# Deformable layer of a four-layer kernel: the first sampling weights are made before the branch, and the first window load is issued from two queues

## The chip, the core and the metric

The kernel runs on one core of a Trainium2 chip as one launch. The metric is the device time of that launch in microseconds (us): 5652.51 us before the change, the median of three runs (5646.67, 5652.51 and 5653.47). A difference of about 0.2% is the smallest that a measurement of this kernel can tell from none.

## What is computed

The reference takes an image batch `x` of shape (2, 128, 128, 128) and adds four layers to it in turn, each behind a normalisation: an axial attention, a scan of nine-tap convolutions in four directions, a deformable 3x3 convolution, and a convolution in a Hadamard-transformed form. Only the third is touched. Cut to what matters:

```
offset, mask = split(conv2d(x, w_off, b_off))      # 27 maps: 9 taps x (dy, dx), and 9 masks
py = off_y + ky + hh ;  px = off_x + kx + ww       # where each tap of each pixel reads
sampled = bilinear(x, py, px) * sigmoid(mask)      # (B, Cin, 9, H, W)
out = einsum('bckhw,ock->bohw', sampled, w) + b    # 3x3 weights, summed over channels and taps
```

## The kernel before, in words

The four layers run one after the other. An image stays in SBUF as `res[n]`, channels on the partitions. The deformable layer (`layer2`, L1166) has two stages and a branch between them.

**Offsets** (`layer2_offsets`, L1180). It first loads the small weights `woff` and `boff` and writes zeros around the padded image `px_d` in HBM with eight transfers, all of them issued by ScalarE's queue (ACT, L1191 to L1205); then it computes the group normalisation, whose square root is on ScalarE too (L45), behind these issues. Then 16 blocks of 16 rows follow: ScalarE normalises the rows into `gx` (L1224), TensorE makes the 27 offset maps (`ps_off`, 36 matmuls, L1236), the maps are transposed (`pt`, `ot`) and written to `off_d` in HBM by SyncE's queue (SP, L1260), the normalised rows are transposed too and written to `px_d`, channels last (L1270). VectorE (DVE) keeps the largest and smallest offset. At the end `far` (L1285) tells whether any offset is beyond 2.

**Branch** (L1173). All five engines read `far` and compare. With far offsets `layer2_gather` would run; with the inputs of this kernel the other side, `layer2_windows`, does.

**Windows** (`layer2_windows`, L1288). The work is 128 halves: 2 images x 32 groups of 4 rows x 2 half-rows of 64 pixels. For a half, ten transfers of 80 KB on SP's queue load `xw`, 16 windows of 10x10 pixels with all channels (L1320), and an eleventh loads the offsets `o` (L1322). From `o` and the constant `base` VectorE and ScalarE make the hats: `hats` (DVE), `hatted` (ACT: Abs, then Relu), `masked` (DVE). Each half is then done in two parts `b`. For a part, `outer` (DVE) multiplies the hats of y and x into `w`, `turn` (PE, nine transposes) and `turned` (DVE copy) bring it to `s`, `sample` (PE, eight matmuls) applies `s` to the windows, `sampled` (ACT copies) brings the samples to `sm`, and `convolve` (PE) multiplies them by `wdef`; `finish` (DVE) adds the result to `res`.

The order within an engine is written by hand: every operation of this stage is recorded through `InOrder` (L73), whose line L81 therefore stands for all of them, and tile names tell them apart. In part `b` the code asks first for `turn` and `turned` of part `b+1` and `outer` of part `b+2`, then, in even parts, for `hats` of the half after the next, and only then for `sample` of part `b`. Each engine takes its instructions strictly in that order: a VectorE instruction that waits for a transfer holds all VectorE instructions behind it.

A transfer is issued under one of eight semaphores, used in turn; an issue waits until the last transfer under the same semaphore has landed, so at most eight transfers of this kind are in flight.

Ahead of the loop come the loads of halves 0 to 2, the hats of halves 0 and 1, and the first `outer`, `turn` and `turned`, in this order:

```
loads = {at: load(at) for at in range(3)}
for at in range(2):
    ds[at] = hats(loads[at][1]); hatted(ds[at]); masked(ds[at], loads[at][1])
w = outer(ds[0], 0); ps_w = turn(w); s = turned(ps_w); w = outer(ds[0], 1)
```

Of the kernel before, what the change touches and what calls it, by code (L numbers as in the profile page):

```python
# [7 lines left out]
F32 = mybir.dt.float32  # L8
I32 = mybir.dt.int32
AF = mybir.ActivationFunctionType  # L10
ALU = mybir.AluOpType
# [1154 lines left out]
def layer2(env, prm, res, mem, tables, st_gn, st_next):  # L1166


    nc, tc = env.nc, env.tc
    with tc.tile_pool(name="l2f", bufs=1) as fp:  # L1170
        far = fp.tile([1, 1], I32, name="far", tag="far")
        layer2_offsets(env, prm, res, mem, st_gn, far)
        is_far = nc.values_load(far[0:1, 0:1])  # L1173
        with tc.If(is_far > 0) as branch:
            layer2_gather(env, prm, res, tables, st_gn, st_next)
        with branch.Else():
            layer2_windows(env, prm, res, mem, st_next)


def layer2_offsets(env, prm, res, mem, st_gn, far):  # L1180
# [5 lines left out]
    with ExitStack() as ctx:  # L1186
# [29 lines left out]
        for n in range(N):  # L1216
            for h in range(0, S, NR):
# [56 lines left out]
                at += 1  # L1274

# [12 lines left out]
def layer2_windows(env, prm, res, mem, st_next):  # L1288

    nc, tc = env.nc, env.tc
    ident = env.ident
    with ExitStack() as ctx:
        cp = ctx.enter_context(tc.tile_pool(name="l2d", bufs=1))
        sp = ctx.enter_context(tc.tile_pool(name="l2s", bufs=2))
        pp = ctx.enter_context(tc.tile_pool(name="l2qs", bufs=1, space=PSUM))
        pe, dve, act = (InOrder(tc, e) for e in (nc.tensor, nc.vector, nc.scalar))
        wdef = cp.tile([P, 9, P], F32, name="wdef", tag="wdef")  # L1300
        nc.scalar.dma_start(out=wdef, in_=prm["wdef"])
        bdef = cp.tile([P, 1], F32, name="bdef", tag="bdef")
        nc.scalar.dma_start(out=bdef, in_=prm["bdef"])
        base = cp.tile([P, 18, 10], F32, name="base", tag="base")
        nc.scalar.dma_start(out=base, in_=prm["base2"])

        px = mem["px"]
        halves = [(n, g, hf) for n in range(N) for g in range(NT) for hf in range(2)]

        def load(at):  # L1310
            n, g, hf = halves[at]
            xw = sp.tile([100, 16, P], F32, name="xw", tag="xw", bufs=4)
            for y in range(10):
                here = px[n, g * RT + y, hf * 64 : hf * 64 + 10, :]
                src = bass.AP(
                    tensor=here.tensor,
                    offset=here.offset,
                    ap=[[P, 10], [4 * P, 16], [1, P]],
                )
                nc.sync.dma_start(out=xw[10 * y : 10 * y + 10], in_=src)  # L1320
            o = sp.tile([P, 2, 27], F32, name="o", tag="o", bufs=4)
            nc.sync.dma_start(out=o, in_=mem["off"][n, g, :, 2 * hf : 2 * hf + 2, :])  # L1322
            return xw, o

        def hats(o):
            d = sp.tile([P, 2, 18, 10], F32, name="d", tag="d")
            dve.tensor_tensor(
                d,
                o[:, :, 0:18].unsqueeze(3).to_broadcast([P, 2, 18, 10]),
                base.unsqueeze(1).to_broadcast([P, 2, 18, 10]),  # L1330
                ALU.add,
            )
            return d

        def hatted(d):
            act.activation(d, d, AF.Abs)
            act.activation(d, d, AF.Relu, bias=1.0, scale=-1.0)

        def masked(d, o):
            rows = d.rearrange("p b (k a) s -> p b k a s", a=2)[:, :, :, 0, :]  # L1340
            dve.tensor_tensor(
                rows, rows, o[:, :, 18:27].unsqueeze(3).to_broadcast([P, 2, 9, 10]), ALU.mult
            )

        def outer(d, b):
            w = sp.tile([P, 9, 10, 10], F32, name="w", tag="w")
            v = d[:, b].rearrange("p (k a) s -> p k a s", a=2)
            dve.tensor_tensor(
                w,
                v[:, :, 0, :].unsqueeze(3).to_broadcast([P, 9, 10, 10]),  # L1350
                v[:, :, 1, :].unsqueeze(2).to_broadcast([P, 9, 10, 10]),
                ALU.mult,
            )
            return w

        def turn(w):
            ps = pp.tile([100, 9, P], F32, name="ps_w", tag="ps_w")
            for k in range(9):
                pe.transpose(ps[:, k, :], w[:, k].rearrange("p y x -> p (y x)"), ident)
            return ps  # L1360

        def turned(ps):

            s = sp.tile([100, 8, 36, 4], F32, name="s", tag="s")
            dve.tensor_copy(
                s.rearrange("p t k c -> p k t c"),
                ps.rearrange("p k (r t c) -> p (k r) t c", r=4, t=8),
            )
            return s

        def sample(xw, s, b):
            ps = pp.tile([P, 3, 512], F32, name="ps_s", tag="ps_s")
            for t in range(8):
                pe.matmul(
                    ps[:, t // 3, (t % 3) * 144 : (t % 3) * 144 + 144],
                    lhsT=xw[:, 8 * b + t, :],
                    rhs=s[:, t].rearrange("p k c -> p (k c)"),
                    start=True,
                    stop=True,
                )  # L1380
            return ps

        def sampled(ps, sm, b):
            for j in range(3):
                nt = (3, 3, 2)[j]
                lo = 8 * b + 3 * j
                act.copy(
                    sm.rearrange("p k (t c) -> p k t c", c=4)[:, :, lo : lo + nt, :],
                    ps[:, j, 0 : nt * 144].rearrange("p (t k c) -> p k t c", t=nt, c=4),
                )  # L1390

        def convolve(sm, po, taps):
            for k in taps:
                pe.matmul(
                    po,
                    lhsT=wdef[:, k, :],
                    rhs=sm[:, 4 * k : 4 * k + 4, :],
                    start=(k == 0),
                    stop=(k == 8),
                )  # L1400

        def finish(at, po):
            n, g, hf = halves[at]
            here = res[n][:, g * RT : g * RT + RT, hf * 64 : hf * 64 + 64]
            dve.scalar_tensor_tensor(here, po, bdef[:, 0:1], here, ALU.add, ALU.add)
            if hf == 1:
                dve.bn_stats(
                    st_next[:, n, g, :],
                    res[n][:, g * RT : g * RT + RT, :].rearrange("p h w -> p (h w)"),
                )  # L1410

        count = len(halves)
        loads = {at: load(at) for at in range(3)}
        ds = {}
        for at in range(2):
            ds[at] = hats(loads[at][1])
            hatted(ds[at])
            masked(ds[at], loads[at][1])  # L1420
        w = outer(ds[0], 0)
        ps_w = turn(w)
        s = turned(ps_w)
        w = outer(ds[0], 1)
        sms, pos = {}, {}
        for b in range(2 * count + 2):
            at, part = b // 2, b % 2
            if part == 0 and at + 3 < count:
                loads[at + 3] = load(at + 3)
            if part == 0 and at < count:  # L1430
                sms[at] = sp.tile([P, 36, 64], F32, name="sm", tag="sm")


            s_now = s
            if b + 1 < 2 * count:
                ps_w = turn(w)
                s = turned(ps_w)
                if b + 2 < 2 * count:
                    w = outer(ds[(b + 2) // 2], b % 2)
            if at + 2 < count:  # L1440
                if part == 0:
                    ds[at + 2] = hats(loads[at + 2][1])
                else:
                    masked(ds[at + 2], loads[at + 2][1])
            if b < 2 * count:
                ps_s = sample(loads[at][0], s_now, part)
                sampled(ps_s, sms[at], part)
                if part == 0 and at + 2 < count:
                    hatted(ds[at + 2])
            if at >= 1:  # L1450
                if part == 0:
                    pos[at - 1] = pp.tile([P, RT, 64], F32, name="po", tag="po_w", bufs=2)
                convolve(sms[at - 1], pos[at - 1], range(0, 5) if part == 0 else range(5, 9))
                if part == 1:
                    finish(at - 1, pos.pop(at - 1))
                    sms.pop(at - 1), loads.pop(at - 1), ds.pop(at - 1)
# [621 lines left out]
```

## Time and profile before

| | us |
|---|---|
| median of three runs | 5652.51 |
| lowest and highest | 5646.67, 5653.47 |
| the profiled execution's own time | 5645.21 |
| its span, first to last instruction | 5643.4 |
| TensorE (PE) busy in the span | 5270.7 |
| offsets stage: first `woff` issue to `far` | 3819.86 to 3999.98 |
| windows stage: first transfer to the last `hats` | 4006.53 to 5260.8 |

How to read the views. A row of the timeline gives the start, the duration, the engine (PE for matmuls, PEld for weight loads, DVE, ACT, POOL; a `q` behind the name is the queue that issues a transfer), the line, the operation, the tiles as out<-in, the shape, how many such instructions follow each other, and in brackets how long the engine had been idle and what ended that. An f32 matmul leaves two records, a transpose one. A row of the stretches gives a window, then each engine's busy time with its instruction count, the TensorE clock that was granted (1.00 is full speed), the busy share of the DMA engines and GB/s.

### The profile page before, as it was taken

Reading aid. Unit: us, or ns where it says so; the run is one execution under the profiler, and the core shown is the slowest. Engines: PE = TensorE matmul, PEld = TensorE weight load, DVE = VectorE, ACT = ScalarE, POOL = GpSimd, SP = SyncE. Lnnn points to the kernel's source line nnn. Section 1 sums busy time; section 2 is a strip of 40 time slices with the busy share of each in tenths; the row PEclk is TensorE's granted clock in tenths of the full one; section 3 lists DMA queues with packets and bytes.
Section 4 is the critical chain, followed back from the end, with each engine's and each line's share of the span. In section 5 each row is a group of like instructions: output and inputs, shape, how many; then the busy total and the mean of one; then the engine's idle time right before and its main releaser. Section 6 shows DMA issues by size and latency. Waiting matters only on the chain. (4 is left out here: it accounts for less than half of the span.)

```text
span 5643.4 us, 164496 instructions
## 1 busy us (share of the span) xinstructions
PE 5270.7 (93%) x68347; PEld 4712.5 (84%) x68347; DVE 3697.0 (66%) x7127; ACT 2648.5 (47%) x7896; POOL 1549.2 (27%) x1169
## 2 busy tenths in 40 slices
PE   8997999999999904999999999999799999999999
PEld 8866888888888704999999999994599999999877
DVE  3645888888888854555555556663466666666698
ACT  1046988898888865443223331003233333333322
POOL 2113666666666622000000002330000000000376
PEclk9998999999999957999999999999899999999999
DMA  3243333333333393000000000103577767777211
GB/s 147 97 186 115 60 59 60 61 62 62 60 60 60 72 377 137 1 1 1 2 1 1 1 1 31 46 24 111 107 88 87 86 90 86 88 89 86 49 50 57
DMA packets 413963, 403.75 MB, mean 72 GB/s; under 512 B 63520, under 2 KB 368544, under 8 KB 402336
## 3 DMA queue, kind: packets, MB, share of 16 engines
q1 hardware_dynamic: 404000, 365.18, 32.0%
q10 hardware_dynamic: 9216, 27.95, 1.3%
q8 instruction: 548, 8.98, 0.7%
q14 instruction: 199, 1.63, 0.1%
HBM read 252.31 MB, written 140.68 MB: 70 GB/s over the span
## 5 line engine op out<-in xcount | busy, mean ns | idle before, releaser
L81 PE MATMUL pl<-ln,wl 128*128 128x128 f32 (+1 forms) x10160 | 1240.6, 276 | 30.5 <-DVE ln L81 30.4
L81 PEld LDWEIGHTS pl<-ln,wl 128*128 128x128 f32 x10160 | 1176.2, 190 | 41.4 <-issue 27.0
L81 ACT ACTIVATE e<-e,mx 128x128 f32<-128x128 f32 x2048 | 793.4, 395 | 0.8 <-DVE mx L81 0.8
L81 ACT COPY sm<-ps_s 128x432 f32<-128x432 f32 (+1 forms) x768 | 318.4, 487 | 801.5 <-PE ps_s L81 801.5
L81 POOL TENSOR_TENSOR e<-e,total 128x1024 f32<-128x1024 f32 x256 | 485.9, 1898 | 476.0 <-DVE total L81 465.5
L81 ACT COPY res<-ln 128x128 f32<-128x128 f32 x762 | 262.3, 344 | 719.2 <-DVE ln L81 719.2
L81 PE MATMUL ps_s<-s,xw 100*128 100x144 f32 x4096 | 546.4, 287 | 0.6 <-ACT sm L81 0.6
L81 POOL TENSOR_TENSOR res<-ln,x1t 128x128 f32<-128x128 f32 x256 | 134.4, 525 | 1494.1 <-DVE ln L81 1494.1
L81 DVE COPY s<-ps_w 100x1152 f32<-100x1152 f32 x256 | 346.4, 1353 | 301.7 <-PE ps_w L81 301.7
L81 PE MATMUL po<-sm,wdef 128*128 128x256 f32 x2304 | 539.1, 379 | 0.0
L81 PE MATMUL pl<-ln,ws 128*128 128x128 f32 x4064 | 536.8, 273 | 0.0
L81 POOL COPY et<-et 128x1024 f32<-128x1024 f32 x256 | 516.9, 2019 | 35.3 <-DVE et L81 27.1
L81 PEld LDWEIGHTS ps_s<-s,xw 100*128 100x128 f32 x4096 | 518.2, 191 | 1.1 <-ACT sm L81 1.1
L81 DVE TENSOR_TENSOR v<-pl,c 128x128 f32<-128x128 f32 x508 | 148.1, 291 | 538.4 <-PE pl L81 538.4
L81 PEld LDWEIGHTS pl<-ln,ws 128*128 128x128 f32 x4064 | 494.5, 190 | 0.0
L81 ACT ACTIVATE r<-gen,alphas 128x1536 f32<-128x1536 f32 x256 | 395.0, 1543 | 171.5 <-PE gen L81 142.7
L81 PEld LDWEIGHTS po<-sm,wdef 128*128 128x128 f32 x2304 | 419.8, 190 | 47.6
L81 POOL MEMSET col<- 128x10 f32 (+1 forms) x72 | 5.9, 122 | 1477.4 <-DVE res L81 1469.9
L81 ACT ACTIVATION_READ_ACCUMULATOR e<-e,mx 128x1 f32 x2048 | 396.1, 193 | 0.0
L81 DVE SCALAR_TENSOR_TENSOR ln<-v,res 128x128 f32<-128x128 f32 x1016 | 343.5, 338 | 49.2 <-DVE v L81 1.2
L81 PE MATMUL te<-cst_main,e 128*128 128x128 f32 x2048 | 338.5, 288 | 24.5 <-POOL e L81 17.3
L81 DVE COPY et<-te 128x512 f32<-128x512 f32 x512 | 348.1, 680 | 11.5 <-PE te L81 10.9
(241 smaller groups left out, 9351.8 us busy)
## 6 DMA issues: line engine op xcount, KB each, us to landing
xw<-px_d SPq DMA_DIRECT2D x1280, 80.0 KB
xa<-in_x SPq DMA_DIRECT2D x16, 1024.0 KB
v_d<-vs SPq DMA_DIRECT2D x16, 1024.0 KB
qb_d<-sb SPq DMA_DIRECT2D x16, 1024.0 KB
qa_d<-sa SPq DMA_DIRECT2D x8, 2048.0 KB
zz<-qb_d SPq DMA_DIRECT2D x1024, 16.0 KB
vt<-v_d SPq DMA_DIRECT2D x64, 256.0 KB
qk<-qa_d SPq DMA_DIRECT2D x256, 64.0 KB
```

Source lines behind the costliest of these rows:

```text
L81: return lambda *a, **k: self.tc.keep_in_program_order(issue(*a, **k))
```

## The change

`layer2_windows` becomes a class `Windows` with three steps. Its constructor runs at the head of `layer2` and holds the tiles that live on both sides of the branch. `begin` is called in the offsets stage, behind the code of its fourth block. `turn_first` stands between the offsets and the read of `far`. `run` is the old stage without what was moved.

```diff
-        layer2_offsets(env, prm, res, mem, st_gn, far)
+        windows = Windows(env, prm, fp)
+        layer2_offsets(env, prm, res, mem, st_gn, far, lambda: windows.begin(mem))
+        windows.turn_first()
         is_far = nc.values_load(far[0:1, 0:1])
...
+                if at == 4:
+                    then()
...
+    def __init__(self, env, prm, fp):
+        self.o = [fp.tile([P, 2, 27], F32, name=f"o{k}", tag=f"o{k}") for k in range(2)]
+        nc.scalar.dma_start(out=self.base, in_=prm["base2"])
+        nc.scalar.dma_start(out=self.wdef, in_=prm["wdef"])
+        nc.scalar.dma_start(out=self.bdef, in_=prm["bdef"])
...
+    def begin(self, mem):
+        for at in range(2):
+            self.env.nc.sync.dma_start(
+                out=self.o[at], in_=mem["off"][0, 0, :, 2 * at : 2 * at + 2, :]
             )
         for at in range(2):
+            self.hatted(self.hats(at, self.o[at]))
+            self.masked(self.d[at], self.o[at])
+        for b in range(2):
+            self.outer(self.d[0], b)
+
+    def turn_first(self):
+        with self.env.tc.tile_pool(name="l2q0", bufs=1, space=PSUM) as pp:
+            self.turned(self.turn(pp, self.w[0]), 0)
...
-                nc.sync.dma_start(out=xw[10 * y : 10 * y + 10], in_=src)
+                    queue = nc.scalar if at == 0 and y % 2 else nc.sync
+                    queue.dma_start(out=xw[10 * y : 10 * y + 10], in_=src)
+                if at < 2:
+                    return xw, self.o[at]
```

The loop over the parts is the same; it starts with `s` and the second `w` at hand. The tiles `d`, `w` and `s` were taken from pools of two buffers and are now two named buffers each. `layer2_gather` takes `wdef` and `bdef` from the class and has fewer buffers; it does not run here.

In the built program the two `o` loads stand on SP's queue behind the `px_d` write of the first block; the six VectorE and four ScalarE instructions of `begin` stand behind the fourth block's copies on VectorE and behind the sixth block's `gx` on ScalarE; the nine transposes of `turn_first` are TensorE's last work ahead of the branch, and its copy is VectorE's last, behind `far`. The loads of `base`, `wdef` and `bdef` stand ahead of `woff`, `boff` and the eight zero writes on ScalarE's queue, under the same eight semaphores: the fourth to eighth zero write then wait for `base`, `wdef`, `bdef`, `woff` and `boff` to land. Behind the branch VectorE has, in order: the copy to `s` of part 1, `outer` of part 2, `hats` of half 2 (which waits for half 2's `o`, the 31st transfer of the stage), the copy to `s` of part 2, `outer` of part 3.

## The prediction on record

> **What bounds the kernel now.** The page says first that TensorE (PE) is busy 93% of the span, so what counts is where it isn't. The line of slices has one such place past the middle, near 4000 us, the seam between offsets and windows. Two stretches, asked for by time, show it:
>
> ```profile
> PE 5270.7 (93%) x68347; PEld 4712.5 (84%) x68347; DVE 3697.0 (66%) x7127; ACT 2648.5 (47%) x7896; POOL 1549.2 (27%) x1169
> ...
> 3999.00:4035.50 36.50, 4.31 (x19) 3.59 (x20) 5.68 (x10) 2.01 (x4) 0.00 (x0) 0.50 0.67 143
> 4035.50:4060.00 24.50, 23.95 (x160) 22.34 (x159) 14.55 (x17) 9.04 (x21) 0.00 (x0) 0.92 0.53 52
> ```
>
> In the first PE works 4.31 of 36.5 us, at half clock (0.50); from the second on it is full, and the stretches from 4060 to 5260 us give 1199.57 of 1200 us. So the windows are PE-bound, at 9.8 us a half, and what starts them earlier ends the kernel earlier. The timeline of the seam, DVE, SP and PE rows taken out:
>
> ```profile
> 3999.84 0.14 DVE L1285 CAST far<-m 1x1 int32<-1x1 f32 x1
> 4006.53 0.34 ACTq L1301 DMA_DIRECT2D wdef<-in_wdef  x1
> 4006.56 9.40 SPq L1320 DMA_DIRECT2D xw<-px_d  x10
> 4016.00 0.35 SPq L1322 DMA_DIRECT2D o<-off_d  x1
> 4016.40 4.55 SPq L1320 DMA_DIRECT2D xw<-px_d  x10
> 4019.72 0.53 DVE L81 TENSOR_TENSOR d<-o,base 128x360 f32<-128x360 f32 x1 [19.74 <-DMA xw<-px_d]
> 4025.83 0.53 DVE L81 TENSOR_TENSOR d<-o,base 128x360 f32<-128x360 f32 x1 [4.12 <-DMA o<-off_d]
> 4027.04 0.34 SPq L1322 DMA_DIRECT2D o<-off_d  x1
> 4028.96 2.13 PE L81 MATMUL ps_w<-cst_main,w 128*100 128x128 f32 x9 [29.64 <-DVE w L81]
> 4035.56 4.03 PE L81 MATMUL ps_s<-s,xw 100*128 100x144 f32 x16
> 4043.11 1.16 PE L81 MATMUL ps_w<-cst_main,w 128*100 128x128 f32 x9
> ```
>
> `far` is known at 3999.98; the branch gives nothing until 4006.5. The first offsets `o` are SP's eleventh transfer and are used at 4019.72, the second at 4025.83; only behind both hats does the first transpose start, at 4028.96. The last row is the third turn of this stage (part 3's weights), and from there PE doesn't pause: I compare both kernels at this instruction.
>
> The head of the layer has a second gap on PE, 3818 to 3828.55 us, which ends with ScalarE's queue:
>
> ```profile
> 3819.86 0.34 ACTq L1191 DMA_DIRECT2D woff<-in_woff  x1
> 3820.23 0.44 ACTq L1193 DMA_DIRECT2D boff<-in_boff  x1
> ...
> 3824.77 0.84 ACTq L1205 DMA_DIRECT2D px_d<-zero  x2
> 3825.66 0.20 ACT L45 ACTIVATE gs_l<-gs_l 128x2 f32<-128x2 f32 x1 [8.99 <-DMA px_d<-zero]
> 3826.29 4.41 ACT L1224 ACTIVATE gx<-res,gb_l,gs_l 128x2176 f32<-128x2176 f32 x2 [0.43 <-DVE gb_l L69]
> ```
>
> The square root at 3825.66 follows the eighth zero write at once: its operand was ready at 3825.22, so ScalarE's issues are last here by 0.44 us.
>
> **What the Trainium skill says.** "DMA: Bandwidth & Descriptors", section "Issuing engines are not separate DMA queues": transfers from SP and ACT run on the same 16 engines, and two issuers save issue time alone. Same page, "Why a DMA increments its semaphore by 16 and not by 1": a transfer uses at most 16 engines, the largest number dividing its slowest dimension, and the lowest-numbered ones; ten partitions give the same ten each time. The trace fits: the DMA share is 0.69 from 4006 to 4028 us, near ten of 16, though nothing there shows two queues loading windows. "TensorE: Matmul & The Clock Gate", "Part 1: The HAM clock gate": half clock after about 3.4 us idle, full after as much work. The trace agrees roughly: 0.50 in the gap, nine transposes 2.13 us there and 1.16 later, the clock back at 4039.4 (its mean is 0.57 from 4036 to 4040). "ScalarE: Activation LUTs", "Table sets": abs and relu are in every set, so the moved hats reload no table; no reload shows at 4020.29 us either, where Abs follows Sigmoid.
>
> **The change part by part.**
>
> *Moved hats, first case.* They take six DVE instructions (2 x 0.53, 2 x 0.35, 2 x 1.09 = 3.9 us) and on ScalarE 2 x 1.04 us in between, about 6.2 us as a chain. They start behind the fourth block's last copy (3872.41 + 1.28 = 3873.7) and end at 3879.9; DVE's next copy is due at 3879.99. Cost 0, hidden by DVE's 6.3 us idle in each block; were the cover gone, DVE would be late by the excess, at most 6 us once. The two `o` loads stand on SP's queue behind the first block's `px_d` write and wait for its `off_d` to land; that was issued at 3840.39, and even the 8.5 us that a transfer needed at its slowest near the seam end ahead of SP's next issue, at 3850.71: 0.
>
> *Turn before the branch.* PE's nine transposes, 2.13 us at the low clock, begin when `far`'s last operand is reduced, near 3999.7; DVE's copy (1.36 us) follows, to about 4003.3. SP, ACT and POOL read `far` as before. PE enters the branch some 2 us later, DVE 3 us, so near 4008 and 4010, both long before the first windows land: 0.
>
> *First load.* `wdef` (576 KB), `bdef` and `base` no longer run beside it; SP waited 3.4, 0.5 and 0.8 us for them. The first `xw` is issued at 4006.5; in an empty queue (fourth load, 4043.18) the first transfer was in after 3.4 us, then one each 0.55 us (ten issues and an `o` in 5.7 us): all ten by 4006.5 + 3.4 + 9 x 0.55 = 4014.9. Halved issue time brings nothing, since 0.4 us an issue is already under 0.55. Sample 0 starts then, 20.6 us earlier than at 4035.56.
>
> *What is late next.* Not all of this arrives. On DVE's queue `hats` of half 2 stands ahead of the copy to `s` of part 2 and `outer` of part 3, and it waits for the third `o`, behind 30 window transfers. The second and third loads take 5.7 us each: 4014.9 + 11.4 = 4026.3; from the distances of the old trace (4019.72 to 4025.83, then 5.97 between `o` issues) it is 4026.2. I take 4026. PE is done with samples 0 and 1 near 4022 and stands. Then hats 0.53, copy 1.3, `outer` 1.09, hand-over 0.1: the third turn starts at 4029.0 against 4043.11, 14.1 us earlier. PE has stood 7 us and is at half clock; for 2.6 to 4.1 us (3828.55 to the rise at 3831.2, by a mean of 0.74 from 3826 to 3836; 4035.3 to 4039.4) it does half: -1.3 to -2.0, I take -1.7. Gain at the seam 12.4 us.
>
> *Head of the layer.* Three issues go ahead of `woff` (0.45 + 0.34 + 0.44, or 1.30 for `bdef` as at 4006.90), of which 0.93 us vanishes in ACT's old wait for the zeros; and the fifth to eighth zero write now wait for `wdef`, `bdef`, `woff`, `boff` to land. At the 240 GB/s that the seam reaches, 576 KB take 2.4 us behind a 2 us start: `wdef` in by 3824.8, `boff` by 3826.3, the eighth zero issued 3826.8, the square root 3827.2 for 3825.66. Cost 1.5, bounds 0.3 (issues alone) and 3.2 (if `wdef` takes its old 6.3 us, 4006.53 to the end of SP's wait at 4012.84). I take 1.8. PE idles all the while.
>
> Sum: 12.4 - 1.8 = 10.6 us. Against the profiled execution 5645.21 - 10.6 = 5634.6; the median shown, 5652.51, is 7.3 above that execution, and gives **5641.9 us**.
>
> **Rivals.** *Wider loads* (0.11): if two queues did reach more engines, or transfers ran at 0.35 us, the third `o` would land near 4019.5 and the gain be 17 us: 5635.5. Only the first ten transfers have two queues, and the share of 0.69 speaks against it.
>
> *Slow loads* (0.14): the transfers issued from 4043.18 took 8.5 us from the fourth `o` (4048.97) to its use (4057.45), about 1 us each. With PE now working beside loads 1 and 2, these may run at 0.9: the third `o` at 4033, gain 10.6 - 7 = 3.6 us: 5648.9. Against: the eighth load is issued in 3.9 us (4071.40 on, against 7.63 for the seventh) under full work.
>
> *Loads become the bound of all windows* (0.05, the slower side): a half needs its eleven transfers in 9.8 us. From 4100 to 5250 us SP waits 343.4 us for PE, some 2.9 us a half, so a load needs 6.9, and it decides only where that passes 9.8; at 10.0 us a half, 125 halves cost 28 us, 17 more than gained: 5670. The tiles lie elsewhere in SBUF, the pattern of transfers is the same.
>
> **How the numbers follow.** A difference under 0.2% (11.3 us) can't be told from none. The forecast (0.70) has 6.5 to 15 us of gain (5637.5 to 5646), a little under half of it over 11.3. Faster: 0.34 + 0.11 = 0.45; same: 0.36 + 0.14 = 0.50; slower 0.05. Range 5636 to 5650.
>
> **What would show it.** Right: `d<-o,base` of half 2 waits for a DMA until about 4026 (in before's time plus the head's delay), the third turn follows 3 us later, and sample 0 runs some 12 us ahead of it. The square root at the head comes 1 to 3 us later than 3825.66. Wrong: no idle PE between samples 1 and 2, a `gx` in block 5 held by hats, or halves over 9.8 us.

## The result and the profile after

The changed kernel takes 5640.34 us (median of 20 runs, 5633.88 to 5646.78); the kernel before, run beside it, 5648.68 us (20 runs, 5641.66 to 5658.36). The ratio is 0.9984, with a 95% interval of 0.9977 to 0.9990, which is 9.0 us less (5.6 to 13). With twenty runs of each kernel the interval lies clear of 1, so less than the 0.2% named at the beginning can be told from none here. In a later series with fifteen new runs of the changed kernel the ratio was 0.9979 (0.9972 to 0.9987). Forecast were 10.6 us, a ratio of 0.9981, and 5641.9 us. The profiled execution took 5633.88 us with a span of 5632.1, for 5645.21 and 5643.4 before: 11.3 us less. It is the shortest of the twenty runs, so this difference says less than the ratio does.

TensorE's line of the page, then the two stretches of the seam that were shown of before:

```profile
PE 5270.6 (94%) x68347; PEld 4712.6 (84%) x68347; DVE 3698.2 (66%) x7127; ACT 2645.8 (47%) x7896; POOL 1548.4 (27%) x1169
```

```profile
3999.00:4035.50 36.50, 17.07 (x90) 15.07 (x89) 12.43 (x21) 3.71 (x9) 0.00 (x0) 0.67 0.64 143
4035.50:4060.00 24.50, 24.50 (x172) 22.98 (x171) 14.63 (x18) 8.93 (x21) 0.00 (x0) 1.00 0.59 84
```

PE does the same work (5270.6 us for 5270.7). In the first stretch it is busy 17.07 us for 4.31, and in the second it no longer pauses. The timeline of the seam, with the DVE, PE and SP rows of one answer:

```profile
4003.09 1.58 PE L81 MATMUL ps_w<-cst_main,w 128*100 128x128 f32 x9 [0.37 <-DVE m L1290]
4003.24 0.14 DVE L1292 CAST far<-m 1x1 int32<-1x1 f32 x1
...
4009.70 1.28 PE L81 MATMUL ps_w<-cst_main,w 128*100 128x128 f32 x5 [5.04 <-issue]
4009.74 14.74 SPq L1401 DMA_DIRECT2D xw<-px_d  x25
...
4013.07 1.09 PE L81 MATMUL ps_w<-cst_main,w 128*100 128x128 f32 x4 [2.09 <-issue]
...
4018.10 4.18 PE L81 MATMUL ps_s<-s,xw 100*128 100x144 f32 x16 [3.94 <-DMA xw<-px_d]
4022.07 2.12 PE L81 MATMUL ps_w<-cst_main,w 128*100 128x128 f32 x9
4023.99 2.24 PE L81 MATMUL ps_s<-s,xw 100*128 100x144 f32 x16
4024.74 0.35 SPq L1405 DMA_DIRECT2D o<-off_d  x1
...
4028.65 0.53 DVE L81 TENSOR_TENSOR d<-o,base 128x360 f32<-128x360 f32 x1 [12.03 <-DMA o<-off_d]
...
4031.60 2.13 PE L81 MATMUL ps_w<-cst_main,w 128*100 128x128 f32 x9 [5.37 <-DVE w L81]
```

The reader should see three waits, one behind the other. Behind the branch PE does five transposes of part 1's turn, stands 2.09 us with nothing shown to wait for ("issue"; the last section comes back to it), and does four more. Then it waits 3.94 us for the first windows. After the samples of parts 0 and 1 it waits 5.37 us for DVE, which itself had waited 12.03 us for the third `o`, the transfer issued at 4024.74. The last row is the turn of part 3's weights, which the prediction and the expectations below call the third turn. The turn of part 4, which follows at 4038.11 (4048.70 before), is from here on the mark at which kernels are compared, because PE runs nearly without a pause behind it.

The head of the layer, ScalarE's rows:

```profile
3820.57 0.33 ACTq L1306 DMA_DIRECT2D base<-in_base  x1
3820.94 0.44 ACTq L1308 DMA_DIRECT2D wdef<-in_wdef  x1
3821.43 0.44 ACTq L1310 DMA_DIRECT2D bdef<-in_bdef  x1
3822.12 0.33 ACTq L1196 DMA_DIRECT2D woff<-in_woff  x1
...
3826.39 1.16 ACTq L1210 DMA_DIRECT2D px_d<-zero  x2
3827.59 0.20 ACT L45 ACTIVATE gs_l<-gs_l 128x2 f32<-128x2 f32 x1 [10.21 <-DMA px_d<-zero]
```

Layer 1 happened to end 0.71 us later in this execution (first issue of the head 3820.57 for 3819.86). Counted from that first issue, the square root comes at 7.02 us for 5.80.

### The profile page after: what moved, and what is told of

It reads as the page before. It is cut to its first block, busy times and chain, and to the rows that moved or that the text cites. A ratio compares the mean times of both kernels' runs of the same rounds, so it can differ in the third digit from the quotient of the medians.

```text
span 5632.1 us, 164505 instructions
## 1 busy us (share of the span) xinstructions
PE 5270.6 (94%) x68347; PEld 4712.6 (84%) x68347; DVE 3698.2 (66%) x7127; ACT 2645.8 (47%) x7896; POOL 1548.4 (27%) x1169
## 5 line engine op out<-in xcount | busy, mean ns | idle before, releaser
L81 DVE COPY et<-te 128x512 f32<-128x512 f32 x512 | 349.0, 682 | 12.8 <-PE te L81 12.4
```

Source lines behind the costliest of these rows:

```text
L81: return lambda *a, **k: self.tc.keep_in_program_order(issue(*a, **k))
```

## The experiments

Every kernel was built from the changed one, except `only_consts`, which is the kernel before with one part of the change. They ran in four series, each beside its own runs of the kernel before. The table has, for each profiled execution: *head* and *far*, from the first issue on ScalarE's queue at the layer's head to the square root and to `far` known; *sample 0* and *turn 4*, from SyncE's first window transfer behind the branch to sample 0 and to the turn of part 4; *sum*, from the head's first issue to the turn of part 4, with the gain on before; and the measured ratio to before with its interval.

| kernel | head | far | sample 0 | turn 4 | sum (gain) | ratio |
|---|---|---|---|---|---|---|
| before | 5.80 | 180.1 | 29.0 | 42.1 | 228.8 | 1 |
| after | 7.02 | 182.8 | 8.4 | 28.4 | 217.5 (11.3) | 0.9984 (0.9977-0.9990) |
| after again | 7.29 | 182.4 | 8.9 | 29.9 | 218.6 (10.3) | 0.9979 (0.9972-0.9987) |
| `one_queue` | 7.05 | 182.5 | 10.0 | 33.6 | 222.6 (6.3) | 0.9983 (0.9975-0.9991) |
| `turn_late` | 7.08 | 182.8 | 9.3 | 30.3 | 219.7 (9.2) | 0.9979 (0.9971-0.9987) |
| `consts_late` | 8.19 | 182.6 | 8.9 | 32.9 | 221.7 (7.2) | 0.9976 (0.9966-0.9985) |
| `only_consts` | 5.80 | 180.6 | 25.2 | 37.1 | 224.3 (4.5) | 0.9988 (0.9981-0.9994) |
| `o2_early` | 7.45 | 182.4 | 9.3 | 22.6 | 211.4 (17.5) | 0.9975 (0.9969-0.9982) |
| `o_early` | 7.30 | 182.1 | 8.2 | 21.7 | 210.1 (18.7) | 0.9970 (0.9959-0.9981) |
| `o_early` again | 7.08 | 182.7 | 8.1 | 21.9 | 211.1 (17.7) | 0.9966 (0.9954-0.9977) |
| `o_head_late` | 5.79 | 181.2 | 9.3 | 22.8 | 210.4 (18.5) | 0.9972 (0.9963-0.9982) |
| `warm` | 6.95 | 182.0 | 8.9 | 21.3 | 209.7 (19.2) | 0.9966 (0.9953-0.9978) |
| `xw_early` | 8.18 | 182.9 | 3.8 | 16.3 | 205.5 (23.4) | 0.9965 (0.9952-0.9979) |
| `xw_head_late` | 5.81 | 180.6 | 3.8 | 16.3 | 203.2 (25.7) | 0.9941 (0.9924-0.9957) |

0.0010 of the ratio is 5.6 us, so the intervals tell steps of 10 us apart and not steps of 2; for those the profile's stretches have to speak, and they come from one execution each.

**The third `o` (`o2_early`, `o_early`).** The theory says that one small transfer, queued 31st, sets the third turn. It is moved ahead of the branch, with the fourth in `o_early` (the diff) or alone in `o2_early` (3 in place of 4 in the second loop and in the condition).

```diff
-        self.o = [fp.tile([P, 2, 27], F32, name=f"o{k}", tag=f"o{k}") for k in range(2)]
+        self.o = [fp.tile([P, 2, 27], F32, name=f"o{k}", tag=f"o{k}") for k in range(4)]
...
-        for at in range(2):
+        for at in range(4):
+            hf = at % 2
...
-                out=self.o[at], in_=mem["off"][0, 0, :, 2 * at : 2 * at + 2, :]
+                out=self.o[at], in_=mem["off"][0, at // 2, :, 2 * hf : 2 * hf + 2, :]
...
-                if at < 2:
-                    return xw, self.o[at]
-                o = sp.tile([P, 2, 27], F32, name="o", tag="o", bufs=4)
+                o = self.o[at % 4]
+                if at < 4:
+                    return xw, o
```

> The changed kernel with the o of half 2 loaded in the offsets stage beside the first two, so that the hats of half 2 wait for no transfer; nothing else differs. Main theory (that o alone sets the third turn): the third turn follows sample 1 at once, 16.5 us after the first window transfer for 21.9, PE keeps its clock there, and the fourth o, in 24.2 us after the first transfer, becomes late by 1 us at most: 5 to 7 us faster than the changed kernel. Rival (the windows themselves are as late as the o): sample 2 waits for the second load, at most 3 us faster.

> The changed kernel with the o of halves 2 and 3 loaded in the offsets stage; nothing else differs. Main theory: as with the o of half 2 alone, and the hats of half 3 wait for no transfer either: PE without a pause from sample 0 on; 6 to 8 us faster than the changed kernel, and at most 1.5 us faster than with half 2 alone. Rival (the windows are as late as the o): sample 2 or 4 waits for its load, at most 3 us faster.

In `o_early` the third turn starts 16.5 us after the first window transfer, in `o2_early` 17.1 us, for 21.9 in the changed kernel. PE rows of `o_early`:

```profile
4018.56 4.18 PE L81 MATMUL ps_s<-s,xw 100*128 100x144 f32 x16 [4.02 <-DMA xw<-px_d]
4022.53 1.86 PE L81 MATMUL ps_w<-cst_main,w 128*100 128x128 f32 x9
4024.23 2.13 PE L81 MATMUL ps_s<-s,xw 100*128 100x144 f32 x16
4026.94 1.16 PE L81 MATMUL ps_w<-cst_main,w 128*100 128x128 f32 x9 [0.58 <-DVE w L81]
```

The 5.37 us wait is down to 0.58, and the turn takes 1.16 us instead of 2.13: PE has kept its clock. With the third `o` alone the fourth is late, as expected, and PE loses 0.83 us for it (DVE and PE rows of `o2_early`):

```profile
4034.53 0.53 DVE L81 TENSOR_TENSOR d<-o,base 128x360 f32<-128x360 f32 x1 [4.59 <-DMA o<-off_d]
...
4037.48 1.16 PE L81 MATMUL ps_w<-cst_main,w 128*100 128x128 f32 x9 [0.83 <-DVE w L81]
```

By medians `o_early` is 6.9 us faster than the changed kernel beside it (5629.03 for 5635.90), as expected, and `o2_early` 4.3 us, a little under the 5 to 7. Between the two lie 2.6 us by the medians and 1.2 us by the stretches, where at most 1.5 was expected. No sample waited for its second or third load, so the rival falls. Once more, with the next two kernels:

> The kernel with the o of halves 2 and 3 loaded in the offsets stage once more, beside the two kernels of this call. From its first run: sample 0 8.2 us and the turn of part 4 21.7 us after the first window transfer, no pause of PE between sample 0 and that turn over 1 us, 0.9970 of the time before (0.996 to 0.998).

It did: sample 0 at 8.1, turn 4 at 21.9 us, the longest pause between them 0.47 us, the ratio 0.9966.

**The first load from one queue (`one_queue`).**

```diff
-                    queue = nc.scalar if at == 0 and y % 2 else nc.sync
+                    queue = nc.sync
```

> The changed kernel with all ten transfers of the first window load on SyncE's queue; nothing else differs. Main theory (the same ten DMA engines take the transfers whoever issues them, one each 0.5 us): sample 0 starts 8.4 us after the first window transfer is issued, as in the changed kernel (18.10 - 9.74), within 0.5 us; the third turn 21.9 us after it, within 0.7; the time within 2 us of the changed kernel. Rival (two queues do bring the first windows sooner): sample 0 at 9.5 to 11 us, the third turn 1 to 3 us later, the time 1 to 3 us longer.

Sample 0 at 10.0 us is what the rival said, the third turn at 25.8 (4042.92 - 4017.16) is later than either said, and the time is the changed kernel's. The profile is no clean witness: in this execution all transfers were slower, those too that have one queue in both kernels. The fourth load (the first row of ten window transfers behind a single `o`), first the changed kernel's, then `one_queue`, then `consts_late`, which has two queues:

```profile
4025.20 4.65 SPq L1401 DMA_DIRECT2D xw<-px_d  x10
```

```profile
4035.81 5.54 SPq L1401 DMA_DIRECT2D xw<-px_d  x10
```

```profile
4027.93 5.91 SPq L1407 DMA_DIRECT2D xw<-px_d  x10
```

Against `consts_late`, which ran at the same slow pace, `one_queue` has sample 0 1.1 us later and the third turn 0.35 us later (25.76 for 25.41). So the second queue may bring the first windows a us sooner, and that us is lost again ahead of the third turn. What the second queue is worth stays open, and so does what sets the pace of an execution.

**The turn ahead of the branch (`turn_late`).**

```diff
-        windows.turn_first()
...
-            s, w = self.s[0], self.w[1]
+            s, w = self.turned(self.turn(pp, self.w[0]), 0), self.w[1]
```

> The changed kernel with the first turn and its copy put back behind the branch, ahead of the loop; hats and outer products stay in the offsets stage. Main theory (the third o sets the third turn, so the turn ahead of the branch is worth nothing): PE and DVE do the first turn and copy within 7 us of the first window transfer, the second turn must wait for that copy and ends near 9.2, so sample 0 comes up to 1 us later than the 8.4 us of the changed kernel, but the third turn stays at 21.9 us within 0.7, and the time within 2 us. Rival (the turn ahead of the branch carries part of the gain): third turn 1.5 to 3.5 us later, and so the time.

The third turn came 22.5 us after the first window transfer (4037.38 - 4014.89), sample 0 at 9.3, the time within 2 us: the turn ahead of the branch is worth nothing as long as the third `o` is late.

**The constants ahead of the layer (`only_consts`).** The kernel before, with the three loads in the place where the changed kernel has them.

```diff
         far = fp.tile([1, 1], I32, name="far", tag="far")
+        base = fp.tile([P, 18, 10], F32, name="base", tag="base")
+        nc.scalar.dma_start(out=base, in_=prm["base2"])
+        wdef = fp.tile([P, 9, P], F32, name="wdef", tag="wdef")
+        nc.scalar.dma_start(out=wdef, in_=prm["wdef"])
+        bdef = fp.tile([P, 1], F32, name="bdef", tag="bdef")
+        nc.scalar.dma_start(out=bdef, in_=prm["bdef"])
         layer2_offsets(env, prm, res, mem, st_gn, far)
```

> The kernel before with one part of the change alone: base, wdef and bdef are loaded at the head of the layer, first on ScalarE's queue; hats, outer products and turns stay behind the branch and all window transfers on one queue. Main theory (SyncE's waits for wdef, bdef and base, 4.7 us, go, and the first two o are used that much sooner; the hats' two waits for o remain): third turn 32 us after the first window transfer, for 36.6 before and 21.9 after, within 1 us; the head 1.2 to 3 us later; the time 1 to 3 us under before. Rival (the loads beside the windows were the whole of it, the moved hats nothing): third turn near 22 us, the time as the changed kernel's. Other rival (the loads cost nothing there): third turn still at 36 us, the time 1 to 3 us over before.

The third turn is 31.7 us after the first transfer (4040.48 - 4008.79), as expected: 4.9 of the 14.7 us by which the change brings it forward are owed to `wdef`, `bdef` and `base` no longer running beside the windows. The other 9.8 are a remainder: they belong to what else was changed, the first two `o`, hats and outer products ahead of the branch (the turn adds nothing, by `turn_late`; the second queue's share is open). The expected loss at the head did not come, for a reason that the trace shows: here the three loads were issued at 2594.8 us, in layer 1. Why they were placed there, and not at the head as in the changed kernel, was not looked into. The square root is at 5.80 us, exactly as before, and the time is 5.5 us under before by medians, for the 1 to 3 expected with a loss at the head. So the loads cost the head nothing when they are done before it begins.

**The constants on another queue (`consts_late`), and held back (`o_head_late`).** Both move the three loads to SP's queue. `consts_late` asks for them behind the code of the first block. `o_head_late` is `o_early` with them, and with three copies of one column of the normalisation's result into the tiles, the loop in this diff, which hold the loads back behind the square root.

```diff
+    def constants(self, prm, gb):
+        nc = self.env.nc
+        for to in (self.base[:, 0, 0:1], self.wdef[:, 0, 0:1], self.bdef):
+            nc.vector.tensor_copy(to, gb[:, 0:1])
+        nc.sync.dma_start(out=self.base, in_=prm["base2"])
+        nc.sync.dma_start(out=self.wdef, in_=prm["wdef"])
+        nc.sync.dma_start(out=self.bdef, in_=prm["bdef"])
```

> The changed kernel with the loads of base, wdef and bdef taken from ScalarE's queue ahead of woff and put on SyncE's queue behind the first block's two writes; nothing else differs. Main theory (these three issues, and the zero writes' waits behind them, hold the square root): the square root comes 5.8 us after the first issue of the head, as before the change, for 7.0 in the changed kernel; TensorE's clock rises some 10 us after its fall as before, not 13.7; far is known 180.1 us after the head's first issue for 182.8; the seam stays as in the changed kernel (third turn 21.9 us after the first window transfer); 1.2 to 2.8 us faster than the changed kernel. Rival (the later offsets are layer 1's and the clock's doing, by chance): the square root 1.2 us earlier, far not earlier by more than 1.2, and the time within 1 us.

This missed. The loads went out at the very same time as `woff`, not behind the first block, and the square root came at 8.2 us, 1.2 later than in the changed kernel:

```profile
3821.53 0.43 SPq L1369 DMA_DIRECT2D wdef<-in_wdef  x1
...
3823.74 1.30 ACTq L1211 DMA_DIRECT2D px_d<-zero  x2
...
3825.37 1.44 ACTq L1206 DMA_DIRECT2D px_d<-zero  x2
...
3826.85 2.44 ACTq L1211 DMA_DIRECT2D px_d<-zero  x2
3829.33 0.20 ACT L45 ACTIVATE gs_l<-gs_l 128x2 f32<-128x2 f32 x1 [11.39 <-DMA px_d<-zero]
```

The pairs of zero writes take 1.30 to 2.44 us to issue, for 0.82 to 0.98 before. In the trace the issues of both queues use the same eight semaphores, and the sixth zero write goes out at 3826.48, as the last part of the transfer under its semaphore lands (3826.46). The longest piece is another: the issue of the seventh takes 1.96 us, though its semaphore was free from 3826.28 on. So waiting for a semaphore explains a part of the delay, and the rest stays open.

> As with the o of halves 2 and 3 early, and base, wdef and bdef are loaded by SyncE's queue behind the layer's group normalisation (three 1-column copies from its result into them hold the loads back), so that ScalarE's queue has woff, boff and the zero writes alone, as before the change. Main theory: the square root 5.8 us after the head's first issue, as before, for 7.0 in the changed kernel; far 180.1 to 181 us after it for 182.8; the seam as with both o early; 8 to 11 us faster than the changed kernel. Rival (the head's later offsets come from the clock's grid alone): the square root 1.2 us earlier but far still 182 us or more after the head's first issue, no gain over both o early.

Held back, the loads leave the head as it was: the square root at 5.79 us, `far` 1.2 us sooner than in the changed kernel beside it (181.2 for 182.4). It still isn't 180.1, since the clock's half rate lasted 13.65 us (see below). The time, 3.0 us under the changed kernel and 3.9 over `o_early`, isn't the expected 8 to 11; the intervals overlap with both, so the times alone tell nothing here.

**The kernel again, the half clock, and the first windows (`after_again`, `warm`, `xw_early`, `xw_head_late`).**

> The changed kernel itself once more, beside the three kernels of this call and for the spread of its own stages. Main theory (ScalarE's three issues and the clock's grid make the head later): far known 182.8 us after the head's first issue, within 0.5, for 180.1 before; half clock at the head 13.7 us again, for 10.2 before. Rival (the later offsets of the first profile were chance): one of the two back at the value of before. The window transfers land one each 0.51 to 0.53 us, or, as two of the four runs so far had it with the same transfers, 0.63 to 0.67; the third turn 21.9 us after the first of them in the one case, 25.5 in the other.

The head's delay is there again (182.4 and 13.65 us), so it was not the chance of one execution; the third turn came at 22.2 us.

`warm` is `o_early` with useless work on PE during its wait for the first windows:

```diff
+                if b == 0:
+                    po = pp.tile([P, RT, 64], F32, name="po", tag="po_w", bufs=2)
+                    flat = po.rearrange("p a c -> p (a c)")
+                    for j in range(16):
+                        pe.transpose(flat[:, 0:128], self.env.ident, self.env.ident)
                 if b < 2 * count:
                     ps_s = sample(loads[at][0], s_now, part)
```

> As with the o of halves 2 and 3 early, and TensorE turns the identity 16 times into an unused PSUM buffer between the second turn and sample 0, while it would wait for the first windows; the extra results are read by nobody. Main theory (the half clock is owed to the wait alone, and costs 3 us between sample 0 and the turn of part 4): sample 0 still 8 to 9 us after the first window transfer, the clock up by 10 us after it for 13.6, the turn of part 4 at 19 to 20.5 us for 21.7, 1 to 2.5 us faster. Rival (the clock follows a grid of its own that the extra work does not reach in time): clock up at 13.6 us as before, no gain.

The clock rose 7.1 us after the first transfer, as the theory had it, but the windows were slow again (issue of a load 5.62 us), PE stood another 1.65 us, and the clock fell for one more stretch of 3.4 us (the clock is the third figure from the end):

```profile
4015.72:4022.80 7.08, 5.42 (x25) 4.93 (x25) 2.81 (x3) 0.00 (x0) 0.00 (x0) 0.50 0.64 128
4023.00:4026.20 3.20, 1.55 (x13) 1.49 (x13) 0.00 (x0) 0.00 (x0) 0.00 (x0) 1.00 0.80 130
4026.40:4029.60 3.20, 3.20 (x16) 3.13 (x15) 0.20 (x1) 2.09 (x5) 0.00 (x0) 0.50 0.78 134
```

Turn 4 at 21.3 us for 21.7 and 21.9, and no gain in time: inconclusive as to the price, since the cover was too short for this execution.

`xw_early` takes the wait away instead: half 0's windows are loaded in the offsets stage (`windows` holds the ten transfers of a load; its last argument spreads them over two queues). Smaller buffers in that stage (`om` and `ot`, one for two) make room, and the branch's other side, which doesn't run, has smaller pools.

```diff
     def begin(self, mem):
...
+        self.windows(mem["px"], self.xw, 0, 0, 0)
...
+                xw = xws[at % 4]
+                if at > 0:
+                    self.windows(px, xw, n, g, hf, at == 1)
```

> As with the o of halves 2 and 3 early, and the ten window transfers of half 0 are issued in the offsets stage as soon as their rows are written; the two queues now share the load of half 1. om and ot of the offsets stage have one buffer for two, and the branch's other side, which does not run, smaller pools. Main theory (with the o early, the first windows alone are what sample 0 waits for): sample 0 4.5 us after the first transfer behind the branch for 8.2, the clock up some 3 us sooner, the turn of part 4 at 17 to 18.5 us for 21.7, 3 to 5 us faster than with both o early. Rival (ten more issues on SyncE's queue, some of them waiting for rows, hold back the writes of offsets behind them): far known 2 us or more later after the head's first issue than 182.5, and no gain.

> The two versions together: half 0's windows and the o of halves 2 and 3 loaded in the offsets stage, and base, wdef and bdef on SyncE's queue behind the group normalisation. Main theory (the head's lateness has two parts, the square root behind ScalarE's longer queue, and one step of the clock's 3.4 us grid that comes or not by a tenth of a us): the square root 5.8 to 6.5 us after the head's first issue for 8.2 with the windows early alone; far 181 to 181.5 us after it if the half clock at the head lasts 13.7 us as in all versions so far but two, 180 if it lasts 10.2; the turn of part 4 16.3 us after the first transfer behind the branch, within 0.7; 1 to 2.5 us faster than with the windows early alone. Rival (nothing at the head counts but the clock's grid): far 182.5 us or more after the head's first issue.

`xw_head_late` adds the held-back constants of `o_head_late`. Its seam:

```profile
4000.05 0.14 DVE L1295 CAST far<-m 1x1 int32<-1x1 f32 x1
...
4006.46 17.37 SPq L1377 DMA_DIRECT2D xw<-px_d  x23
4009.38 1.09 PE L81 MATMUL ps_w<-cst_main,w 128*100 128x128 f32 x4 [1.81 <-issue]
4010.27 3.36 PE L81 MATMUL ps_s<-s,xw 100*128 100x144 f32 x16
...
4013.46 1.15 PE L81 MATMUL ps_w<-cst_main,w 128*100 128x128 f32 x9
...
4017.16 1.16 PE L81 MATMUL ps_w<-cst_main,w 128*100 128x128 f32 x9
...
4022.79 1.15 PE L81 MATMUL ps_w<-cst_main,w 128*100 128x128 f32 x9
```

In both, sample 0 follows the turn at once, and turn 4 stands 16.3 us behind the first transfer, 5.4 us sooner than in `o_early`. `xw_early` loses 0.9 us at the head (8.18 us: here too the issue of the seventh zero write is long, 1.85 us, while SP's queue begins on the windows; the cause was not tested), and its time is 2.0 us under `o_early` beside it, less than the expected 3 to 5 and within the intervals. `xw_head_late`, with the head at 5.81 us, is the fastest version found: 5621.75 us for 5653.04 of before beside it, ratio 0.9941 (0.9924 to 0.9957). Its interval lies under those of before and of the changed kernel. Its stretches explain 25.7 us of the 31 that the medians show; the interval of the ratio is 24 to 43 us. Over `xw_early` it gains 2.3 us by the stretches, within the expected 1 to 2.5.

## Why the prediction was right

The forecast was 10.6 us, and the two profiles of the changed kernel give 11.3 and 10.3 us at turn 4 from the head's first issue; by the ratio it is 9.0 (5.6 to 13). Some of the closeness is luck. The forecast of 5641.9 us started from a median of three runs, 3.8 us above that of all twenty. And a gain under 0.2% was given 0.50 and one above it 0.45: with 0.16% in the first series and 0.21% in the later one, either could have come. Step by step:

*Moved hats, first case*, cost 0: right. DVE began them at 3877.47 and ended the second outer product at 3883.36; the next copy of the offsets stage followed at 3883.50, as due. The whole lateness of `far` is accounted for by the head.

*Turn before the branch*, cost 0: right. SyncE's first window transfer came 6.4 us after `far`, for 6.6 before. By `turn_late` the turn gains nothing either. Not foreseen was that PE would stand 2.09 us in the middle of the next turn, with no releaser in the profile; the wait for the windows hid that.

*First load*: right. It was to be in 8.4 us after its first issue, and sample 0 started 8.4 and 8.9 us after it.

*What is late next*: right in mechanism and size. The third `o` was to be used 19.5 us after the first transfer and the third turn to start at 22.5. Measured were 18.9 and 19.2 (4029.77 - 4010.56), and 21.9 and 22.2. `o2_early` and `o_early` show that it was this transfer and no other. Two terms inside were off and small. PE stood 5.4 us for the 7 predicted: the turn between samples 0 and 1 ran at half clock too (2.12 us, for 1.17 before), and the third turn came 0.6 us sooner. The half clock behind the wait lasted 3.4 us in one profile and 6.8 in the other. PE worked in 2.9 and 5.4 us of it, a loss of 1.4 or 2.7 us for the 1.7 taken. The seam's gain from first transfer to turn 4 is 13.8 and 12.2 us for the 12.4 predicted. (The load at 4043.18 and the `o` at 4048.97, which the prediction calls the fourth, are the fifth of the old trace; the times read from them stand.)

*Head of the layer*, 1.8 us taken, 0.3 to 3.2 as bounds: this is the term that was mis-sized. It measured 2.7 and 2.2 us; in the first profile the seam's 1.4 us more than forecast made up for it. The queue itself cost 1.2 and 1.5 us at the square root, close to the 1.5 worked out. "PE idles all the while" was then taken to mean that a delay costs its own length. It does not: the clock comes back on a grid. The half rate lasted 10.24 us before and 13.65 us after, and one more step of 3.41 us at half rate costs 1.7 us where PE has work in all of it. That step need not be the change's doing alone. In its one profile the kernel before was at most 0.08 us from the same step (last section), and `o_head_late`, whose square root comes as in before, paid it: 13.65 us of half rate. Where in the grid layer 1 ends differs between executions; the head's first issue stood 0.6 to 2.3 us ahead of the clock's fall in the fourteen profiles. How often the kernel before pays the step is not known, so what the change costs the head on average stays open.

The rivals: *Wider loads* fell, transfers landed one each 0.5 us with two queues. *Loads become the bound* fell: from 4060 to 5240 us PE is busy 1180.00 of 1180.00 us. *Slow loads* happens in some executions: three profiles of other versions had the load issued in 5.5 to 5.9 us for 4.65, and in the two of them where the third `o` was still queued the third turn came 3.5 to 3.9 us later than in the changed kernel, half of the 7 that this rival had priced. The two profiles of the changed kernel were not slow; before was profiled once, so whether the change has a part in it is not shown.

## What to carry to other kernels

A wait that is removed uncovers the next one in the same in-order queue: look for the smallest transfer behind the largest ones, here 27 KB behind 2.4 MB, and load it where the queue is empty; that brought another 7 us here. A load without a dependence may be placed elsewhere than it is written, in one version 1.2 ms early, in another at the head, where the zero writes of another queue then went out later; tie it to what it has to follow. To a delay of an idle TensorE add, as a bound, what one more step of its clock at half rate costs, 1.7 us here.

## What the runs showed of the hardware

The granted clock in the traces' records changes on a grid of 3.41 us, which fits "TensorE: Matmul & The Clock Gate", "Part 1: The HAM clock gate" of the Trainium skill: a free-running window of 4096 cycles. At the head PE's first matmul of the offset maps came 7.56 us after the clock's fall in before, and the half rate lasted three steps, 10.24 us. In the changed kernel it came at 7.64 us, and the half rate lasted four, 13.65 us. All fourteen profiles agree: three steps at 6.60, 6.66 and 7.56 us, four at 7.64, 7.68 and above. So 2.68 us of work in a step were enough there and 2.60 were not, and 0.08 us decided over 1.7.

This is no general limit. Behind the branch 2.71 us in the changed kernel and 2.80 in `o_early` again did not raise the clock at the end of the step, and 3.20 in `only_consts` did. What else counts is open. The third step at the head of before and of the changed kernel, then the step behind the branch of the changed kernel:

```profile
3827.81:3831.22 3.41, 2.68 (x16) 0.71 (x20) 0.00 (x0) 2.89 (x2) 0.00 (x0) 0.50 0.01 4
3829.66:3833.07 3.41, 2.60 (x16) 0.63 (x20) 0.00 (x0) 2.96 (x2) 0.00 (x0) 0.50 0.02 6
4017.39:4020.81 3.41, 2.71 (x11) 2.74 (x12) 0.00 (x0) 0.00 (x0) 0.00 (x0) 0.50 0.73 157
```

`warm` shows two things more. A step full of transposes alone (4019.46 to 4022.87) raised the clock, and the next step, with 1.76 us of work, was followed by half rate: no whole idle step was needed.

From `far` to the first transfer behind the branch it takes 6.2 to 6.6 us in all versions, and in all that enter with the turn of part 1 PE stands another 1.4 to 2.3 us within its first nine transposes, with no releaser in the profile but "issue". The trace has more on both. Reading `far` takes an engine about 1.1 us, and PE's compare-and-branch then lasts 4.3 to 4.6 us in all fourteen profiles. The trace also has transfers of instructions, two of 16 KB on one queue behind the branch in the changed kernel, from 3.5 and from 6.8 us after `far` (packets, MB and share of the DMA engines from 4003 to 4014 us):

```profile
q8 instruction: 2, 0.03, 1.5%
```

In all fourteen the compare-and-branch ends 1.36 to 1.39 us after the first of these has ended, and where PE enters with the turn of part 1, its pause ends 1.2 to 1.5 us after the second. So PE seems to wait for instructions at both places. Which engine a transfer serves is not in the trace, and no version moved them, so this is read from the times alone.
